# Graph attention on one core: the second layer's transposes, projection and sums in another order and in other PSUM banks

## Chip, cores and metric

The kernel runs on one core of a Trainium2 chip. The metric is the device time of one execution in microseconds (us); the time of a kernel is the median of its runs. The engines are TensorE (PE, with its weight loads shown as PEld), VectorE (DVE), ScalarE (ACT), GpSimd (POOL) and SyncE (SP); PE writes its results to PSUM[...].

## What is computed

Two graph attention layers, each with a residual and a layer norm, over 3327 nodes with 1024 features and a sparse symmetric adjacency matrix. The second layer has one head:

```python
    def _L1_gnn_ref(input, adj, W, a1, a2):
        h = input @ W
        f1 = h @ a1
        f2 = h @ a2
        e = jax.nn.leaky_relu(f1 + f2.T, negative_slope=ALPHA)
        scores = jnp.where(adj > 0, e, neg)
        attention = jax.nn.softmax(scores, axis=1)
        h_prime = attention @ h
        return jax.nn.relu(h_prime)
    ...
    x = _layernorm(x + _L0_gnn_ref(x, adj, L0_gnn_W, L0_gnn_a_src, L0_gnn_a_dst), axis=-1)
    x = _layernorm(x + _L1_gnn_ref(x, adj, L1_gnn_W, L1_gnn_a1, L1_gnn_a2), axis=-1)
```

The first layer (`_L0_gnn_ref`) is the same with eight heads of 128 features, without the relu.

## The kernel before, in words

The nodes are padded to 26 tiles of 128. The kernel has three stages. The first (0 to about 450 us) projects x with W of layer 0 and finds the edges of each node as lists of indices. The second is layer 0, the third layer 1; both are run by the function `pipeline`, over 26 tiles of target nodes. Everything stands in the order in which the program issues it (`manual_schedule`): no scheduler reorders it. Each engine runs its own instructions in that order, and the waits between engines come from what each instruction reads and writes. A PSUM tile is followed as a whole in these waits: L981 on DVE waits for L951 on ACT although the two touch different slices of `way`.

For each tile the edges come in five steps, b = 0 to 4. Steps 0 to 3 hold four groups of 128 edges each, every group for 32 targets; step 4 (`end`) holds one group of 128 edges for all 128 targets. One step of layer 1's class `Target` consists of:

- `fetch` (L803 in `gather`): indirect DMAs, issued by POOL, that gather the source nodes' rows of `y_d` into one of five buffers `src` (or two buffers `end`), four per step and one for the end. The next tile's step b is fetched just after this tile's sums of step b.
- `weights` (L981, L982, L984, DVE): the edges' attention weights, computed in the PSUM tile `way`, result in `es`. They are computed one step ahead of the sums.
- `sums` (L993, PE): `es` times the gathered rows, accumulated in three PSUM tiles `acc` (the columns are cut in three, taken in the order 2, 0, 1). The profile counts a float32 matmul twice: 24 per step, 6 for the end.

Once in a tile, in step 2, `prepare` makes the next tile's row R: PE transposes the nodes' scores (L949), ACT takes the exponential into a slice of `way` (L951), DVE marks the targets (L819, L823) and SP loads the tile's own rows `y` (L956). At the start of the next tile `close` (L1001 to L1010) divides the sums by the row sums and gives `z`.

What remains of a tile, `finish`, is a generator and is run in pieces between the sums of the next tile: four transposes of `z` and ACT's copy into `xT` (L176 and L179 in `transposed`) as the first piece, the other four as the second, and then per half of the output columns the eight products with W in four pieces (L1025; two products, in the profile's count four, per piece), followed by L1028 on DVE, which takes the relu and adds the residual. The layer norm of the output is a second generator, `settle` (L192 to L199, with a square root on ACT for which ACT loads another table, and the store L1036), and runs in the queue `ahead`.

`pipeline(kind, late, behind, get)` says how many pieces run where: `behind[b]` pieces after the sums of step b, and `late` pieces after `close`, just ahead of the sums of step 0. A tile has 10 pieces. So that the first tile's pieces fall in the same places as the others', a dummy of `range(1)` stands ahead of it in the queue.

PSUM's eight banks are given out by tag in `Phase`: A (5) for the sums of both layers, S (1) for layer 0's row sums `den` and for the projection's result `mm`, T (1) for all transposes, E (1) for `way`. `way` has 512 columns: two slices of 128 for R of this and the next tile, a third for the weights, and a fourth that layer 1 doesn't use.

Of the kernel before, what the change touches and what calls it, by code (L numbers as in the profile page):

```python
# [19 lines left out]
P = 128  # L20
# [6 lines left out]
def kernel(  # L27
# [49 lines left out]
    CUTS = (0, 342, 684, D + 1)  # L77
# [79 lines left out]
    class Phase:  # L157
# [7 lines left out]
        def bank(self, tag, shape, name, dt=F32):  # L165
            return self.psum.tile(shape, dt, tag=tag, name=name, bufs=self.banks[tag])
# [286 lines left out]
    with ExitStack() as own, tc.manual_schedule():  # L453
        ph = Phase(own, "proj", {"A": 2, "S": 1, "T": 2})
        pool, bank = ph.pool, ph.bank
# [205 lines left out]
        for t in range(3, NT):  # L661
# [3 lines left out]
            if t == 12:  # L665
                n, own = NT - 1, pool.tile([P, NT], I32, bufs=1, name="own")
# [27 lines left out]
        tr = bank("T", [1, P], "trc")  # L694
# [46 lines left out]


    def sparse(own):
        ph = Phase(own, "sparse", {"A": 5, "S": 1, "T": 1, "E": 1})
        pool, bank, sbuf = ph.pool, ph.bank, ph.sbuf
        NS = 5
        srcs = [pool.tile([P, NG, HG], F32, bufs=1, name=f"src{n}") for n in range(NS)]
# [8 lines left out]
        way = bank("E", [P, HALF], "way")  # L756
# [30 lines left out]
        def run(work, steps=1):  # L787

            while work and steps:
                try:  # L790
                    next(work[0])
                    steps -= 1
                except StopIteration:
                    work.popleft()
# [19 lines left out]
        def marks(t):  # L814

            m = NB - 1
            oh = sbuf("oh", [P, m * GT + P], 2)
            parts = oh[:, : m * GT].rearrange("p (b t) -> p b t", t=GT), oh[:, m * GT :]
            nc.vector.tensor_tensor(  # L819
                parts[0], io_t[:, :GT].unsqueeze(1).to_broadcast([P, m, GT]),  # L820
                tgt[:, t, :m].unsqueeze(2).to_broadcast([P, m, GT]), OP.is_equal,
            )
            nc.vector.tensor_scalar(parts[1], io_t, tgt[:, t, m:], None, op0=OP.is_equal)  # L823
            return parts

        class Layer0:
# [5 lines left out]
            def prepare(self):  # L832
                self.re = listed.pop(self.t)
                self.oh, self.oh2 = marks(self.t)
                self.y = ys[self.t % 3]
                load_rows(self.y[:, :D], x, self.t)
                self.h = sbuf("own", [P, HW0], 2)
                nc.sync.dma_start(self.h, h0_d[self.t * P : (self.t + 1) * P, :])
# [13 lines left out]
            def begin(self):  # L852
                self.acc = [bank("A", [P, 4, DH], "acc") for _ in range(2)]
# [86 lines left out]
        class Target:  # L940
# [4 lines left out]

            def prepare(self):
                t = self.t
                tr = bank("T", [P, P], "tr")
                nc.tensor.transpose(tr, r1.s[:, t, :].to_broadcast([P, P]), ident)  # L949
                self.r = way[:, (t % 2) * P : (t % 2 + 1) * P].rearrange("p (g t) -> p g t", g=NG)  # L950
                nc.scalar.activation(  # L951
                    self.r.rearrange("p g t -> p (g t)"), tr, AF.Exp, scale=1 - SLOPE
                )
                self.oh, self.oh2 = marks(t)
                self.res = ys[t % 3]
                nc.sync.dma_start(self.res, y_d[t * P : (t + 1) * P, :])  # L956
# [12 lines left out]
                self.src[b] = gather(y_d, HW, self.t, b)  # L969

            def begin(self):
                self.acc = [bank("A", [P, CUTS[1]], "acc1") for _ in range(3)]

            def weights(self, b):
                s = self.src[b]
# [62 lines left out]
        def pipeline(kind, late, behind, get):  # L1038

            tiles = [kind(t) for t in range(NT)]
            work = deque()
            get(0)
            tiles[0].prepare()
            for b in range(EB + 1):
                tiles[0].fetch(b)
            tiles[0].weights(0)
            for t, tg in enumerate(tiles):  # L1050
                tg.begin()
                for b in range(EB + 1):
                    if b == 0 and t:
                        tiles[t - 1].close()
                        run(work, late)
                    if b == 0 and t + 1 < NT:
                        get(t + 1)
                    if b == 2 and t + 1 < NT:
                        tiles[t + 1].prepare()
                    if b == 0:  # L1060
                        tg.own()
                    if b < EB:
                        tg.weights(b + 1)
                    elif t + 1 < NT:
                        tiles[t + 1].weights(0)
                    tg.sums(b)
                    if t + 1 < NT:
                        tiles[t + 1].fetch(b)
                    run(work, behind[b])
                    if t or b:  # L1070
                        run(ahead)
                if t == 0 and late:
                    work.append(iter(range(1)))
                work.append(tg.finish())
            tiles[-1].close()
            run(work, late)
            run(ahead, -1)
            run(work, -1)
            run(ahead, -1)

        with tc.manual_schedule():
            pipeline(Layer0, 0, (1, 1, 1, 1, 1), get_edges)
            pipeline(Target, 1, (2, 2, 2, 2, 1), lambda t: None)


    def by_pairs(own):
# [119 lines left out]
    with arm.Else():  # L1206
        with ExitStack() as own:
            sparse(own)
# [23 lines left out]
```

## Time and profile before

| | us |
|---|---|
| median of 3 runs (lowest to highest) | 1957.28 (1956.42 to 1968.05) |
| the profiled execution | 1903.19 |
| its span, first to last instruction | 1901.5 |
| PE busy | 1518.5 (80%) |
| DVE busy | 1146.6 (60%) |
| POOL busy | 1030.2 (54%) |
| ACT busy | 546.6 (29%) |
| L1025, layer 1's projection on PE | 383.3 |
| L993, layer 1's sums on PE | 206.2 |
| L803, gathers of y_d on POOL | 415.7 |

The profile is one execution on the chip. The span is what its records cover, and the execution's own time lies 1.7 us above it; the median of the runs lies 54.1 us above that. A row of the timeline gives start, duration, engine, line, operation, written and read tiles, and in brackets how long the engine stood idle ahead of it and which instruction's end released it. The chain of waits follows the work that ended last back from the end: each piece is either an instruction or what it waited for. Counts in a row are those of the hardware's instructions.

### The profile page before, as it was taken

What the parts mean: (1) busy time and instruction counts of PE and PEld (TensorE: products, weight loads), DVE (VectorE), ACT (ScalarE), POOL (GpSimd) and SP (SyncE); (2) the same over time, 40 slices, a digit from 0 to 9 for tenths busy, and PEclk for the clock granted to TensorE, in tenths of its full rate; (3) what the DMA queues carried; (4) which work ended last, traced back from release to release, by engine and by line L of the source; (5) the groups of instructions that cost most, each with busy time, mean ns of one, the idle gap of its engine ahead of it and who ended that gap; (6) DMA issues with size and microseconds to landing.
All of it is one profiled execution on the core that took longest, in us unless ns stands there. A gap on an engine that the chain in (4) does not pass through costs nothing.

```text
span 1901.5 us, 38079 instructions
## 1 busy us (share of the span) xinstructions
PE 1518.5 (80%) x14663; PEld 902.4 (47%) x14663; DVE 1146.6 (60%) x3058; ACT 546.6 (29%) x1422; POOL 1030.2 (54%) x1391
## 2 busy tenths in 40 slices
PE   8799999999266555656556565399999999999997
PEld 5465556666255554545545454144444444444443
DVE  6699999986386665666666666244444444444442
ACT  5544455542022222222222222012222212222220
POOL 4322222220576666676676764677766667666650
PEclk9899999999678777787788877699999999999999
DMA  7656455411899999999999997899999999999980
GB/s 184 101 133 131 100 99 99 88 62 39 325 373 404 396 392 394 366 405 392 386 392 389 394 376 273 332 398 410 400 372 382 380 378 369 359 371 373 366 326 33
DMA packets 171068, 567.76 MB, mean 299 GB/s; under 512 B 27690, under 2 KB 34346, under 8 KB 170878
## 3 DMA queue, kind: packets, MB, share of 16 engines
q0 software_dynamic: 131056, 455.68, 67.6%
q1 hardware_dynamic: 39822, 109.56, 15.4%
q8 instruction: 118, 1.93, 0.4%
q14 instruction: 72, 0.59, 0.1%
HBM read 578.85 MB, written 42.97 MB: 327 GB/s over the span
## 4 chain that ended last, share of the span: by engine, by line
PE 52%; DMA 24%; DVE 12%; ACT 6%; issue 4%; POOL 2%; SPq 0%; DVEq 0%; ACTq 0%; POOLq 0%
DMA src<-h_d,idx 20%; PE mm L1025 20%; PE acc L993 12%; PE mm L479 12%; DVE e L870 3%; PE acc L898 3%; ACT junk L311 3%; PE tr L176 2%; POOL src L803 2%; DMA src<-y_d,idx 2%; DVE pr L931 1%; PE acc L882 1%; DMA wt<-in_L_gnn_W_dram 1%; ACT xT L179 1%; PE xp L411 1%
## 5 line engine op out<-in xcount | busy, mean ns | idle before, releaser
L803 POOL DMA_INDIRECT src<-h_d,idx x416 | 441.1, 1060 | 209.1 <-PE acc L898 58.0
L803 POOL DMA_INDIRECT src<-y_d,idx x416 | 415.7, 999 | 221.6 <-PE acc L993 96.3
L898 PE MATMUL acc<-src,e 128*32 128x128 f32 x6656 | 278.5, 337 | 253.6 <-DVE e L870 253.5
L479 PE MATMUL mm<-wt,xT 128*128 128x347 f32 (+1 forms) x1248 | 402.3, 469 | 3.3 <-DMA wt<-in_L_gnn_W_dram 2.9
L1025 PE MATMUL mm<-wt,xT 128*128 128x512 f32 x832 | 383.3, 604 | 0.8 <-DVE o L1028 0.8
L898 PEld LDWEIGHTS acc<-src,e 128*32 128x32 f32 x6656 | 234.8, 137 | 311.3 <-DVE e L870 284.3
L479 PEld LDWEIGHTS mm<-wt,xT 128*128 128x128 f32 x1248 | 228.3, 192 | 106.0 <-issue 4.2
L1025 PEld LDWEIGHTS mm<-wt,xT 128*128 128x128 f32 x832 | 152.2, 190 | 199.5 <-issue 179.1
L993 PE MATMUL acc<-src,es 128*32 128x342 f32 (+1 forms) x2496 | 206.2, 464 | 33.8 <-DVE es L984 31.0
L870 DVE TENSOR_TENSOR e<-oh,way 128x1024 f32<-128x1024 f32 x130 | 158.7, 1221 | 63.2 <-ACT w L868 62.8
L993 PEld LDWEIGHTS acc<-src,es 128*32 128x32 f32 x2496 | 71.6, 111 | 158.6 <-issue 112.9
L868 ACT ACTIVATE w<-way 128x32 f32<-128x32 f32 (+1 forms) x130 | 24.6, 189 | 407.7 <-DVE way L866 395.6
L1028 DVE SCALAR_TENSOR_TENSOR o<-mm,y 128x512 f32<-128x512 f32 x52 | 35.9, 691 | 166.2 <-PE mm L1025 166.2
L1007 ACT ACTIVATE z<-y,ri 128x342 f32<-128x342 f32 (+1 forms) x78 | 39.5, 570 | 313.9 <-DVE ri L1003 313.9
L865 DVE TENSOR_TENSOR way<-src,re 128x32 f32<-128x32 f32 x104 | 20.8, 200 | 175.1 <-DMA src<-h_d,idx 157.6
L179 ACT ACTIVATE xT<-tr 128x512 f32<-128x512 f32 x104 | 59.4, 596 | 151.0 <-PE tr L176 150.9
L981 DVE TENSOR_TENSOR way<-way,src 128x128 f32<-128x128 f32 x104 | 31.1, 299 | 90.0 <-ACT way L951 44.2
L850 ACT ACTIVATE own<-own,es 128x128 f32<-128x128 f32 x208 | 63.6, 388 | 57.4 <-DVE es L847 57.4
L311 ACT ACTIVATE junk<-ad 128x3328 uint8<-128x3328 uint8 x26 | 78.4, 3014 | 2.5 <-POOL ad L308 2.5
L882 PE MATMUL acc<-end,e 128*128 128x128 f32 x416 | 67.7, 328 | 13.3 <-DVE e L870 13.3
L296 POOL CAST mvs<-r 128x8 bf16<-128x8 f32 x26 | 6.0, 232 | 122.8 <-ACT r L295 122.8
L335 POOL TENSOR_TENSOR place_of<-cnt 128x1 f32<-128x1 f32 x26 | 4.9, 190 | 121.0 <-ACT cnt L328 101.5
(188 smaller groups left out, 1959.7 us busy)
## 6 DMA issues: line engine op xcount, KB each, us to landing
h_d<-ht SPq DMA_DIRECT2D x26, 520.0 KB
own<-h_d SPq DMA_DIRECT2D x26, 520.0 KB
y_d<-y SPq DMA_DIRECT2D x26, 514.0 KB
y<-y_d SPq DMA_DIRECT2D x26, 514.0 KB
x<-in_x_dram SPq DMA_DIRECT2D x25, 512.0 KB
y<-in_x_dram SPq DMA_DIRECT2D x25, 512.0 KB
out_dram<-o SPq DMA_DIRECT2D x25, 512.0 KB
ad<-in_adj_dram POOLq DMA_DIRECT2D x25, 415.9 KB
```

The source lines that it names most:

```text
L176: nc.tensor.transpose(tr[:, k, :], src[:, (4 * g + k) * P : (4 * g + k + 1) * P], ident)
L179: nc.scalar.activation(part, tr, AF.Copy)
L311: nc.scalar.activation(junk, ad, AF.Copy, accum_out=self.deg)
L479: nc.tensor.matmul(acc, xT[t][:, k, :], wt[:, k, CUTS0[c] : CUTS0[c + 1]], start=k == 0, stop=k == KT - 1)
L803: nc.gpsimd.indirect_dma_start(out=s[:, g, :w], out_offset=None, in_=table[:, :], in_offset=bass.IndirectOffsetOnAxis(ap=idx[:, t, b * NG ...
L850: nc.scalar.activation(hn, hn, AF.Copy, scale=es[:, n : n + 1])
L870: nc.vector.tensor_tensor(e, oh.unsqueeze(2).to_broadcast([P, ng, H, wide]), wp.unsqueeze(3).to_broadcast([P, ng, H, wide]), OP.mult,)
L882: nc.tensor.matmul(self.acc[h // 4][:, h % 4, :], e[:, 0, h, :], rowsof[:, 0, h, :], start=False, stop=h % 4 == 3,)
L898: nc.tensor.matmul(self.acc[h // 4][g * GT : (g + 1) * GT, h % 4, :], e[:, g, h, :], rowsof[:, g, h, :], start=first and h % 4 == 0, stop= ...
L993: nc.tensor.matmul(self.acc[c][to, :m], es[:, g, :], s[:, g, CUTS[c] : CUTS[c + 1]], start=b == 0, stop=b == EB,)
L1007: nc.scalar.activation(z[:, cut], self.res[:, cut], AF.Copy, scale=ri[:, 1:2])
L1025: nc.tensor.matmul(acc, xT[:, k, :], wt1[:, k, half], start=k == 0, stop=k == KT - 1)
```

## The change

It has five edits, in layer 1 but for the banks, which both layers share. The bank counts become 4 for A and 2 for S. R's transpose writes the unused fourth slice of `way` in place of a bank T tile. The three `acc` tiles are taken in the order in which the sums use them. The pieces are spread as `late` 2 and `behind` (1, 1, 2, 2, 2) in place of 1 and (2, 2, 2, 2, 1): the two halves of the transposes now fall behind the sums of steps 0 and 1, the first half of the projection behind those of steps 2 and 3, the second behind the end and ahead of the next tile's sums. The dummy is as long as `late`.

```diff
     def sparse(own):
-        ph = Phase(own, "sparse", {"A": 5, "S": 1, "T": 1, "E": 1})
+        ph = Phase(own, "sparse", {"A": 4, "S": 2, "T": 1, "E": 1})
...
             def prepare(self):
                 t = self.t
-                tr = bank("T", [P, P], "tr")
+                tr = way[:, 3 * P :]
                 nc.tensor.transpose(tr, r1.s[:, t, :].to_broadcast([P, P]), ident)
...
             def begin(self):
-                self.acc = [bank("A", [P, CUTS[1]], "acc1") for _ in range(3)]
+                self.acc = {c: bank("A", [P, CUTS[1]], "acc1") for c in (2, 0, 1)}
...
                 if t == 0 and late:
-                    work.append(iter(range(1)))
+                    work.append(iter(range(late)))
                 work.append(tg.finish())
...
             pipeline(Layer0, 0, (1, 1, 1, 1, 1), get_edges)
-            pipeline(Target, 1, (2, 2, 2, 2, 1), lambda t: None)
+            pipeline(Target, 2, (1, 1, 2, 2, 2), lambda t: None)
```

## The prediction, on record before the changed kernel ran

> **What bounds the kernel now.** I began with the busy time by window, to see which stage the edited lines lie in (columns: window, length, busy time and count of PE, PE weight loads, DVE, ACT, POOL, then granted clock, DMA share, GB/s):
>
> ```profile
> 450.00:1198.00 748.00, 444.23 (x8282) 364.49 (x8280) 467.28 (x1135) 176.90 (x525) 469.00 (x449) 0.79 0.94 362
> 1198.00:1260.00 62.00, 40.16 (x250) 15.54 (x251) 16.48 (x54) 4.95 (x12) 47.12 (x48) 0.81 1.01 396
> 1260.00:1847.50 587.50, 571.67 (x3294) 245.37 (x3295) 261.88 (x759) 134.27 (x230) 394.31 (x395) 1.00 0.99 378
> 1847.50:1901.50 54.00, 41.57 (x183) 17.89 (x182) 16.71 (x43) 5.69 (x11) 0.00 (x0) 0.94 0.08 30
> ```
>
> Layer 1 is the last three rows. From 1260 to 1847.5 PE is busy for 571.67 of 587.50 us; before that, for some two tiles, it is not. Next the chain of work that ended last, for tile 2 of layer 1; its period is the same in every later tile (start us, us, what):
>
> ```profile
> 1260.04 1.86 PE acc L993 x24
> 1261.90 0.60 PE tr L176 x4
> 1262.50 0.02 issue
> 1262.53 0.61 ACT xT L179
> 1263.13 0.04 issue
> 1263.18 0.66 PE tr L176 x4
> 1263.83 1.86 PE acc L993 x24
> 1265.69 3.63 PE mm L1025 x8
> 1269.33 0.11 PE tr L949
> 1269.44 1.86 PE acc L993 x24
> 1271.30 3.63 PE mm L1025 x8
> 1274.93 1.86 PE acc L993 x24
> 1276.79 3.63 PE mm L1025 x8
> 1280.42 1.73 PE acc L993 x6
> 1282.15 3.43 PE mm L1025 x8
> 1285.58 1.86 PE acc L993 x24
> ```
>
> The period is 1285.58 - 1260.04 = 25.54 us. All of it is PE except 0.02 + 0.61 + 0.04 = 0.67: the second half's transposes wait until ACT has emptied the one T bank. Also, eight projection matmuls cost 3.63 after a block of sums with 32-column weights, but 3.43 after the end block. The waits of PE in that window are one row, so nothing else is to be had there:
>
> ```profile
> PE tr L176 <- ACT xT L179: 15.8, 23, 0.7
> ```
>
> Last, the timeline around the start of layer 1 and in the tail (start, duration, [idle before, releaser]):
>
> ```profile
> 1242.37 0.30 DVE L981 TENSOR_TENSOR way<-way,src 128x128 f32<-128x128 f32 x1 [4.20 <-DMA src<-y_d,idx]
> 1876.65 8.73 PE L1025 MATMUL mm<-wt,xT 128*128 128x512 f32 x16
> 1886.16 7.13 PE L1025 MATMUL mm<-wt,xT 128*128 128x512 f32 x16 [0.79 <-DVE o L1028]
> ```
>
> In tile 1 the weights still wait for gathers (4.20); in the tail the second half's matmuls wait 0.79 for the only S bank.
>
> [...] DVE L981 waits 44.2 us in 23 times for ACT L951, although the two use different slices of way. So the moved R transpose must wait for DVE's last use of way. [...] clock records of 3.41 us at 0.5, one of them right after an idle of 2.75 in the tail. [...] The trace has the 1.28 us, and the next ACTIVATE 0.01 us after it; I use 1.28.
>
> **The change, part by part.** T is the start of a tile's first sums.
>
> *Order on PE.* The built order of the changed kernel gives, per tile: sums0, 4 transposes, sums1, 4 transposes, R, sums2, mm8, sums3, mm8, end, mm16 (in the profile's count). With the rows above: 1.86 + 0.60 + 1.86 + 0.60 + 0.11 + 1.86 + 3.63 + 1.86 + 3.63 + 1.73 + 3.43 + 3.42 = 24.59 us. (The final eight follow their like: 8 x 0.427 = 3.42.) Saved: 25.54 - 24.59 = 0.95, say 0.94: 0.67 of ACT wait, 0.06 of the transposes after it, 0.21 because one changeover less has the 0.2.
>
> *Is the wait really covered?* The first half's transposes end at T + 2.46, ACT takes 0.61: free at 3.1. The second half's start at 4.32, behind sums1 (1.86). Cover to spare 1.2. Should it go, 0.67 comes back.
>
> *ACT.* Its order becomes xT half, sqrt table load, sqrt, xT half, exp table load, L951. Second xT half at 4.96 to 5.56, the exp load (which in the built program now waits for the R transpose) 5.56 to 6.84, L951 to 7.1. The second half is needed at the second mm8, T + 12.4: free of charge. DVE's weights for step 3, which wait for L951, run 7.15 to 8.1 (three of 0.3 us); sums3 wants them at 10.5. Before, they ran from T + 9.8.
>
> *R's transpose in way's bank.* New wait: L949 behind DVE's weights for step 2. Queued behind it on PE is sums2, which needs the same weights, so only their lateness counts. The timeline of one tile of before (T = 1515.47, less 0.07 for what the chain calls start) has:
>
> ```profile
> 1519.81 0.29 DVE L984 TENSOR_TENSOR es<-way,oh 128x128 f32<-128x128 f32 x1
> ```
>
> That ends at T + 4.63; DVE's order up to there does not change, and it starts from the last L1028, which still runs at T. PE wants it at T + 4.92: margin 0.29, less some 0.05 of semaphore. Cost 0; if 0.3 us were missing, 7 us in all. Sums1 needs its weights at 2.46, they end at 2.02.
>
> *Two S banks.* In steady state one bank was never waited for (0.8 us, once, in the tail). In the new order only the 1.73 of the end block lies between the halves, L1028 takes 0.69: no wait either way. In the tail the 0.79 goes.
>
> *Four A banks.* A tile takes three, so the next tile's second and third bank are those of which close reads the first and second. Close ends about 4.5 us after the end block starts; the 16 matmuls behind it last until 8.6. Cost 0 (before, too, one bank was shared). Layer 0 takes two per tile: four suffice. Its den rows show no PE wait that a second S bank could remove: 0.
>
> *L1028 of the first half* moves ahead of the next tile's first weights on DVE, which are wanted 7 us later: 0.
>
> *POOL and SP* keep their order. A gather waits for the sums five slots earlier; those now end 0, 1.4, 4.4, 4.4 us earlier in the tile, while src1 is wanted at the same T + 1.1, src2 at T + 3.7, src3 2.5 us earlier. From the landings of each gather in the trace, the slack to its weights is 7.5 to 13 us from tile 9 on; in tile 3 it is 3.8, 1.3 and 2.2 for src1 to src3. One tile takes 17 issues of 1.30 = 22.1 us of POOL, and in bytes about 378 GB/s x 25.5 us = 9.6 MB, which at the 410 seen in early tiles is 23.5 us (estimate). Both are under 24.59. The y load moves with prepare, 2.5 us earlier in the tile; SP has room.
>
> *The start.* Tile 1 is paced by landings: src2 lands at 1242.2, its weights end at 1243.3. Before, PE filled 1240.15 to 1243.78 with mm8. Now it has only four transposes (to 1240.8) and idles 2.6 us; the mm8 comes after the end block. So: sums2 1243.5, mm8, sums3 1249.0, mm8, end 1254.5, mm16 from 1256.2, tile 2 at 1263.1 instead of 1260.04: 3.1 us lost. By the grid of the clock records the window 1239.2 to 1242.6 would be 45% busy. One at 39% was followed by half clock, one at 57% not, so half clock for 3.4 us is open: 0 to 1.7 us more. I take 0.85. Slack after that: tile 3's src3 lands at 1293.1 and is wanted at 1287.7 + 7.3 = 1295.0; later tiles have more.
>
> *Sum.* 24 periods (tiles 2 to 25) x 0.94 = 22.6; start -3.1 and -0.85; tail +0.8. Net 19.4: span 1901.5 to 1882.1, profiled execution 1903.19 to 1883.8. The runs' median lies 54.1 us above that execution, and nothing in the profile shows where; I carry the difference over unscaled: 1957.28 - 19.4 = 1937.9, which is 0.99% less. One per cent, 19.6 us, is about what a measurement of this kernel can tell from no change, so the forecast sits on that line.
>
> **The rivals.**
> *Transfers take over.* DMA share is 0.99 and the runs are slower than the profile. For it: 23.5 us against 24.59 is 4% of room; if the missing 54 us are slow transfers in layer 0's 748 us (7%), a tile costs 25.1 in transfers and gains 0.4, while the start's loss drowns in the wait for them: 24 x 0.4 + 0.8 = 10.4 us, 1947. Against it: in the profile slack grows from tile to tile.
> *The clean sum without the clock loss, or with a longer one:* 1937.0 or 1938.7; part of the forecast.
> *A thin margin fails.* R's wait or sums1's weights lie 0.1 to 0.5 us late, as any delay on DVE passes the 0.24 left: 2 to 12 us given back, 1940 to 1950.
> *Slower.* The same place, further out: if PE's wait for way also covered weights or table loads behind step 2 (L951's exp load, 1.28, or weights 3), each R would hold PE by over a microsecond. It decides from 0.94 + 0.24 = 1.2 us late; at 2.2 us, 24 us lost, 1981. Against it: the built order has only DVE's count on L949, and what stands behind it there doesn't come before.
> *The change does nothing:* PE's order does change, and no other engine has the 0.67 waiting; I give it nothing apart from these.
>
> **How the numbers follow.** Forecast 0.70 (1935 to 1942 with the scatter of the runs), transfers 0.12, thin margin 0.12, slower 0.06. The forecast is over 1% faster about two times in three given that scatter and the unknown clock: 0.47, and with a little of the rest 0.48. Slower 0.06, the remaining 0.46 within. Range 1927 to 1950: it leaves out the slower case and the ends of the others; below, as much as the scatter and a few tenths per changeover (0.2 x 24 = 5 us) could give.
>
> **What would show it.** PE's row "tr L176 <- ACT xT L179" gone but in the tail; a period of 24.6 in the chain; ACT L951 at T + 7; tile 2 starting at about 1263 to 1265; the 0.79 before the last 16 matmuls gone. Wrong if L949 or sums1 shows a DVE wait in each tile, if DVE L981 waits for gathers after tile 5, or if the period stays above 25.

## The result and the profile after

| | before | changed |
|---|---|---|
| median of 6 runs each, first comparison | 1960.4 us | 1991.67 us |
| ratio (95% interval) | | 1.0172 (1.0147 to 1.0198) |
| profiled execution | 1903.19 us | 1988.58 us |
| its span | 1901.5 us | 1986.5 us |

The changed kernel was 1.7% slower in the first comparison; forecast was 1% faster. The table holds a clue to the cause: for the changed kernel the profiled execution agrees with the runs, for the kernel before it lies 57 us under them. The two profiles may therefore not show the same conditions, and cannot simply be subtracted.

The busy time by window of the changed kernel (columns as before):

```profile
450.00:1198.00 748.00, 562.65 (x7948) 384.83 (x7946) 442.91 (x1088) 170.70 (x515) 465.50 (x452) 0.82 0.96 357
1260.00:1847.50 587.50, 552.08 (x3034) 234.26 (x3034) 237.80 (x699) 120.70 (x210) 367.29 (x369) 0.98 0.94 351
```

The first row is layer 0, where the order of the instructions is the same as before: PE is nonetheless busy for 562.65 us instead of 444.23 with fewer matmuls done (7948 against 8282), and layer 1's first gather is issued at 1231.2 us instead of 1198.6. In layer 1, the chain of waits shows a tile's time:

```profile
1500.20 1.86 PE acc L993 x24
1502.06 0.59 PE tr L176 x4
1502.65 1.86 PE acc L993 x24
1504.51 0.59 PE tr L176 x4
1505.10 0.11 PE way L949
...
1517.92 6.87 PE mm L1025 x16
1524.79 1.29 PE acc L993 x16
```

From 1500.20 to 1524.79 the tile runs as forecast, in 24.59 us: the wait for ACT between the transposes is gone and nothing waits for R. But of the 23 tiles from tile 2 to tile 24 it is the only one that does; their mean period is 27.2 us. The loss of the others lies, with few exceptions, in one place: the sums of step 3, the fourth block of sums, and the end of the products just ahead of it. In the tile that begins at 1364.29 that block reads:

```profile
1374.86 0.77 PE acc L993 x7
1375.69 0.45 PE acc L993
1376.13 0.28 issue
1376.41 0.75 PE acc L993 x2
1377.16 0.65 issue
1377.81 1.40 PE acc L993 x14
```

Here matmuls stand apart within a block, with "issue" between them: the engine waits for nothing that the profile shows. Such pauses are called stalls below. In layer 0, where no line of the change stands, the chain of the changed kernel has them too:

```profile
1196.06 0.27 PE acc L898
1196.33 0.46 issue
1196.79 0.28 PE acc L898
```

Between two successive matmuls of L898 more than 0.25 us pass 389 times in the trace of the changed kernel, start to start, and never in the profile of before.

### The profile page after: what moved, and what is told of

Same layout as the page of the kernel before. It is cut to its first block, busy times and chain, and to the rows that moved or that the text cites. A ratio compares the mean times of both kernels' runs of the same rounds, so it can differ in the third digit from the quotient of the medians.

```text
span 1986.5 us, 38080 instructions
## 1 busy us (share of the span) xinstructions
PE 1686.6 (85%) x14663; PEld 950.4 (48%) x14663; DVE 1140.5 (57%) x3058; ACT 545.9 (27%) x1422; POOL 1025.5 (52%) x1391
## 4 chain that ended last, share of the span: by engine, by line
PE 73%; issue 11%; DVE 6%; ACT 5%; DMA 4%; POOL 1%; another core or an unknown queue 0%; DVEq 0%; SPq 0%; POOLq 0%; ACTq 0%
PE mm L1025 17%; PE acc L898 17%; PE acc L993 13%; PE mm L479 12%; PE acc L882 5%; PE acc L890 3%; ACT junk L311 3%; PE tr L176 2%; DMA src<-h_d,idx 2%; DMA wt<-in_L_gnn_W_dram 1%; PE den L907 1%; PE xp L411 1%; DMA src<-y_d,idx 1%; DVE st L192 1%; ACT away L384 0%
## 5 line engine op out<-in xcount | busy, mean ns | idle before, releaser
L803 POOL DMA_INDIRECT src<-h_d,idx x416 | 436.4, 1049 | 241.1 <-PE acc L898 105.1
L898 PE MATMUL acc<-src,e 128*32 128x128 f32 x6656 | 377.8, 306 | 165.8 <-issue 154.4
L898 PEld LDWEIGHTS acc<-src,e 128*32 128x32 f32 x6656 | 238.0, 122 | 321.0 <-issue 280.1
L1025 PE MATMUL mm<-wt,xT 128*128 128x512 f32 x832 | 375.6, 600 | 0.0
L993 PE MATMUL acc<-src,es 128*32 128x342 f32 (+1 forms) x2496 | 242.9, 469 | 70.0 <-issue 37.0
L993 PEld LDWEIGHTS acc<-src,es 128*32 128x32 f32 x2496 | 80.7, 111 | 213.5 <-issue 179.0
L882 PE MATMUL acc<-end,e 128*128 128x128 f32 x416 | 94.3, 418 | 1.6 <-DVE e L870 1.6
L882 PEld LDWEIGHTS acc<-end,e 128*128 128x128 f32 x416 | 87.5, 320 | 2.3 <-DVE e L870 1.7
L890 PE MATMUL acc<-own,ident 128*128 128x512 f32 x104 | 69.7, 757 | 0.0
```

What stands on the lines that cost most here:

```text
L803: nc.gpsimd.indirect_dma_start(out=s[:, g, :w], out_offset=None, in_=table[:, :], in_offset=bass.IndirectOffsetOnAxis(ap=idx[:, t, b * NG ...
L882: nc.tensor.matmul(self.acc[h // 4][:, h % 4, :], e[:, 0, h, :], rowsof[:, 0, h, :], start=False, stop=h % 4 == 3,)
L890: nc.tensor.matmul(self.acc[b - 1].rearrange("p h d -> p (h d)"), ident, self.h[:, (b - 1) * HALF : b * HALF], start=False, stop=False,)
L898: nc.tensor.matmul(self.acc[h // 4][g * GT : (g + 1) * GT, h % 4, :], e[:, g, h, :], rowsof[:, g, h, :], start=first and h % 4 == 0, stop= ...
L993: nc.tensor.matmul(self.acc[c][to, :m], es[:, g, :], s[:, g, CUTS[c] : CUTS[c + 1]], start=b == 0, stop=b == EB,)
L1025: nc.tensor.matmul(acc, xT[:, k, :], wt1[:, k, half], start=k == 0, stop=k == KT - 1)
```

## The experiments

Three theories stood at the start. **A:** the new order of the pieces stalls PE. **B:** the banks, or R in way's bank, do it. **C** (D in later texts): the stalls belong to the chip that a run came to, and the profile of before was of another one. The runs came to several chips, and the kernel before, which ran beside each, took a median of 1898 to 1905 us on three of them (called the first kind below: chips 0, 4, 6) and of 1959 to 1984 on three others (the second kind: chips 7, 8, 10); the first comparison, at 1960, looks like the second. Chip 4 came up twice, half an hour apart, and was of the first kind both times; each other chip came up once, so whether the kind belongs to the chip or to its state at that time is not shown. A period is the mean of the 23 from tile 2 to tile 25. Two further theories on the stalls came later: **T**, they hang on the gathers, and **N**, on the density of short PE instructions.

**Before again, and the change in parts (chip 4).** `e0_before` is the kernel before.

> The kernel before, unchanged, for a profile beside those of the changed kernels. Theory C (the profile of before that the prediction rested on is quicker than that kernel's usual runs, and the stalls of PE without a releaser are in it too): a profiled execution near 1955 us, not 1903, with the additional 50 us in PE rows that name no releaser, in layer 0 or 1. Theories A and B (the stalls come with the change): near 1903 in the profile, tile period 25.5 us in layer 1, no such stalls. Ratio 1.00 within half a per cent in either.

Measured: 1897.34 us, 0.9995 (0.9985 to 1.0005), profiled 1897.84; period 25.5 us, no stalls. The profile of before was no lucky execution: it shows what the kernel does on a chip of this kind. The numbers are those expected of A and B, but the kernel's other runs on this chip took 1898 us too, where the first comparison had 1960: before itself differs between chips by 60 us, which no branch had foreseen.

`e1_banks`, on the changed kernel:

```diff
-            pipeline(Target, 2, (1, 1, 2, 2, 2), lambda t: None)
+            pipeline(Target, 1, (2, 2, 2, 2, 1), lambda t: None)
```

> The changed kernel with the pieces placed as before (late 1, behind 2,2,2,2,1): only the banks, R in way's bank and the order of acc are changed. Theory A (the order of the pieces makes the loss): ratio 1.00 to before, within 0.5%. Theory B (the banks make it: the second S bank or the four A banks delay layer 0, or R in way's bank delays layer 1): 1.010 to 1.017, with layer 0 ending up to 30 us later than in before's run of this job.

Measured: 0.9995 (0.9986 to 1.0004), period 25.5. Banks and R's place alone cost and give nothing on this chip.

`e2_pieces`, on the kernel before:

```diff
-                    work.append(iter(range(1)))
+                    work.append(iter(range(late)))
...
-            pipeline(Target, 1, (2, 2, 2, 2, 1), lambda t: None)
+            pipeline(Target, 2, (1, 1, 2, 2, 2), lambda t: None)
```

> The kernel before with the changed kernel's places of the pieces (late 2, behind 1,1,2,2,2) and a dummy as long as late, but with five A banks, one S bank, R in the T bank. R then waits for ACT's second copy, about 0.7 us per tile, 17 us in all. Theory A: as slow as the changed kernel or slower, ratio 1.015 to 1.025, layer 0 as in before. Theory B: 1.00, that is the 0.7 per tile regained in R and nothing lost.

Measured: 1.0009 (1.0000 to 1.0018). The period stays 25.5: PE's only wait row in layer 1 is now that of R for ACT's second copy,

```profile
PE tr L949 <- ACT xT L179: 15.8, 23, 0.7
```

with the same 15.8 us as the one it replaces. The parts work only together: the split frees PE of the wait, and with R's place in way's bank it does not come back at L949 (in `h_after`, below, PE has no wait row between 1260 and 1835 us). Theory A's loss of 1.5 to 2.5% did not come; but as no kernel stalls on this chip, these runs do not yet decide between A and B.

`e3_even`, on the changed kernel:

```diff
-            pipeline(Target, 2, (1, 1, 2, 2, 2), lambda t: None)
+            pipeline(Target, 2, (1, 3, 2, 2, 0), lambda t: None)
```

> The changed kernel with pieces at late 2, behind 1,3,2,2,0: halves of the transposes still in different steps, but eight projection products after each of the steps 1, 2, 3 and the end, as before, in place of sixteen in one stretch. Theory A (sums and gathers crowd in the first part of a tile and the stretch of sixteen leaves the buffers unemptied): the period is 24.8 us, ratio 0.99. Theory B: as the changed kernel, 1.01 to 1.02. Theory C: the same stalls as in before, ratio 0.99 to 1.00.

Measured: 1871.71 us against 1898.18, 0.9852 (0.9833 to 0.9870), period 24.59: the fastest of the complete kernels on this chip.

**The changed kernel on both kinds of chip.** `g_after` (the changed kernel), `g_even` (as e3_even) and `g_before` (before) came to chip 7.

> The changed kernel again, unchanged. Theory D (a state of the chip or of the program's place in memory, in which PE is without instructions for a while: it was there in the first comparison, where the kernel before too ran at 1957 us against 1898 in the last job): where the kernel before runs at about 1900, the changed kernel has a period of 24.6 us in layer 1, no stalls without a releaser, and a ratio of 0.986 to 0.990. Theory A (the stretch of sixteen, or the crowding of sums, stalls PE by itself): a period near 27.1 and a ratio of 1.01 to 1.02 on this chip as well.

> The same as e3_even, for a comparison on the same chip as g_after. Theory D: 0.985 where before runs at 1900, within 0.3% of the changed kernel; if the chip is one where before runs at 1957, a smaller gain or a loss, like the changed kernel's. Theory A: 0.985, and clearly below the changed kernel.

> The kernel before, for a profile from the same chip as the other two. Theory D: at 1900 us no stalls of PE without a releaser in layer 1; at 1957 us such stalls in its profile too, of some 2 us per tile or in layer 0. Theory A: none, on either chip.

Measured: before 1959.14; changed 1992.84, 1.0163 (1.0134 to 1.0191), period 27.3; g_even 1959.53, 1.0006 (0.9989 to 1.0023), period 26.0; g_before 1.0003 (0.9989 to 1.0017), its period 25.76. All three reach layer 1's first gather at 1231.0 to 1233.1, against 1191.1 to 1195.5 for the four kernels on chip 4: some 37 us of the 60 by which this chip is slower are lost ahead of layer 1, and not through the change. In the 23 periods g_before loses 5.0 us against e0_before, nearly all in three tiles; g_even loses 32.4 against e3_even, g_after 61.1 against the same kernel on chip 4 (`h_after`, next). PE's waits in g_before between 1290 and 1840 us seem to hold, beside the known one, one that names nothing:

```profile
PE tr L176 <- issue: 9.6, 14, 0.7
PE tr L176 <- ACT xT L179: 6.3, 7, 1.4
```

The two rows are most likely one wait: together 21 times, once a tile, with mostly the same 0.7 us. On a chip of this kind part of the records that name a releaser is missing (in the trace of the first comparison 822 of ACT's 1128 counts are there, in the profile of before 1115), so a wait that names nothing is not yet a stall. Pauses within a block of matmuls, as above, have no such wait ahead of them.

`h_after`, the changed kernel on chip 4, and `i_after` on chip 0, with `i_pieces` (as e2_pieces):

> The changed kernel once more. On a chip on which the kernel before takes about 1898, theory D (the loss belongs to chips on which PE also stalls in layer 0) gives a period of 24.6 us and a ratio of 0.986 to 0.990; theory A (the order stalls PE on any chip) 1.01 to 1.02. On a chip on which before takes 1957 both give 1.015 again.

> The changed kernel, as the measure for the other three on the same chip: 1.016 and a period of 27.2 where before takes 1957, 0.989 and 24.6 where it takes 1900.

> As e2_pieces (the changed kernel's places of the pieces, the banks of before, R in the T bank). On a chip where before takes 1957: if the order alone brings the stalls, a period of 27 to 28 and a ratio of 1.016 to 1.025; if they come with R in way's bank, 25.5 to 26 and 1.00. Where before takes 1900: 1.001 again.

Measured: h_after 1883.40 against 1903.98, 0.9889 (0.9870 to 0.9908), period 24.64, no stalls; i_after 0.9922 (0.9905 to 0.9940), 24.62; i_pieces 1.0037 (1.0025 to 1.0050), 25.49. Theory D's branch held, though i_after and i_pieces came out 0.3% higher than expected: the same program is 0.8 to 1.1% faster on one kind of chip and 1.6% slower on the other. A as stated, a loss on any chip, has fallen; so has B. But on a chip of the second kind neither e1_banks nor e2_pieces ever ran. That the order plays a part there follows from g_even and g_after, which have the same banks; whether the banks or R's place add to it is not known.

**What the stalls hang on.** In `few`, layer 1's sums become one matmul per cut (the rest of the line as before):

```diff
-                    for g in range(NG if b < EB else 1):
-                        to = slice(g * GT, (g + 1) * GT) if b < EB else slice(0, P)
                         nc.tensor.matmul(
-                            self.acc[c][to, :m], es[:, g, :], s[:, g, CUTS[c] : CUTS[c + 1]],
+                            self.acc[c][:, :m], es.rearrange("p g t -> p (g t)"), s[:, 0, CUTS[c] : CUTS[c + 1]],
```

In `quarter`, layer 1 gathers one group per step:

```diff
-            for g in range(NG if b < EB else 1):
+            for g in range((NG if w == HW0 else 1) if b < EB else 1):
                 nc.gpsimd.indirect_dma_start(
```

> The changed kernel, but layer 1's sums use the first of the four gathered groups alone, as one matmul with 128 columns of weights in place of four with 32: the sums of the other three groups are left out. PE's time for a step stays (1.73 us against 1.86), its instructions for it fall from 24 weight loads and 24 matmuls to 6 and 6; all gathers are still made. On a chip with stalls, theory N ([...] three steps of sums follow one another with only transposes between) expects the stalls gone and a period of 24.0 to 24.3 us. Theory T (the transfers of the gathers hold PE up) expects the period to stay at 27. On a chip without stalls, 24.0 to 24.3 in both.

> The changed kernel with only one of the four groups of each step gathered in layer 1: three quarters of the rows are left out, and what an earlier gather left in the buffers is used in their place. On a chip with stalls, theory T expects them gone, a period of 24.6 us. Theory N expects them to stay, a period of 27. On a chip without stalls, 24.6 in both, and tile 1 without its wait for gathers.

> As h_few (layer 1's sums of three of the four groups left out, one matmul with 128 columns of weights in place of four with 32; all gathers made). On a chip where before takes 1957: theory N (too many short instructions in a burst) a period of 24 us in layer 1; theory T (the transfers) a period of 26.5 to 27. On a chip where before takes 1900: 23.9 again, which tells nothing.

> As h_quarter (three of the four groups of each step are not gathered in layer 1; older rows are used). On a chip where before takes 1957: theory T a period of 24.6 us; theory N 27. On a chip where before takes 1900: 24.6 again.

> As h_few (layer 1's sums of three of the four groups left out; a quarter of PE's short instructions, all gathers made). On a chip where before takes 1957: theory N (dense short PE instructions) a period near 24 us and the stalls gone in layer 1; theory T (the gathers, their transfers or the records of their landings) 26.5 to 27. On a chip where before takes 1900: 23.9.

> As h_quarter (three of four groups not gathered in layer 1, older rows used; all PE instructions). On a chip where before takes 1957: theory T 24.6 us per tile and all records of landings there in layer 1; theory N 27. On a chip where before takes 1900: 24.6.

These six came to chips 4, 0 and 6, of the first kind, and so settled nothing about the stalls. `few`: 0.9813 (0.9791 to 0.9836), 0.9812 (0.9793 to 0.9832), 0.9806 (0.9730 to 0.9882), period 23.97. `quarter`: 0.9766 (0.9746 to 0.9786), 0.9775 (0.9755 to 0.9795), 0.9781 (0.9714 to 0.9848), period 24.59, tile 1 without its wait. That `quarter` has the changed kernel's period (24.59 against 24.64 and 24.62) with a DMA share of 0.39 instead of 0.98 (h_quarter and h_after, 1260 to 1847.5) says that on these chips transfers don't set it.

`k_quarter`, the same as h_quarter, came to chip 8, of the second kind:

> As h_quarter (three of four groups not gathered in layer 1, older rows used; all PE instructions). On a chip where before takes 1957: theory T (gathers, their transfers or the records of their landings) a period of 24.6 us; theory N (dense short PE instructions) 27. On a chip where before takes 1900: 24.6.

Measured: 1907.67 against 1983.71, 0.9599 (0.9503 to 0.9695), period 24.59 in every tile, no stall in layer 1, while layer 0, untouched, has them as on chip 7 (PE busy for 544.37 us from 450 to 1198; g_after 557.41, h_after 444.02). T's branch held, and N falls as it was stated: all short instructions of the sums were there, and without the gathers they bring no stall. That their density plays no part is not shown: `few` never came to a chip of the second kind, and there g_before, g_even and g_after, with the same gathers and the same instructions, lose 5.0, 32.4 and 61.1 us; they differ in their order and, the first from the other two, in the banks.

`l_narrow` keeps all gathers and cuts their bytes to a quarter:

```diff
+            if w == HW:
+                w, table = HW // 4, table[:, :].rearrange("n (a w) -> (n a) w", a=4)
+            else:
+                table = table[:, :]
...
-                    out=s[:, g, :w], out_offset=None, in_=table[:, :],
+                    out=s[:, g, :w], out_offset=None, in_=table,
```

> The changed kernel with all of layer 1's gathers, each moving 257 instead of 1028 elements per row (rows cut to a quarter and taken from other places; the rest of the buffer is older data). On a chip where before takes 1957 or more: if the stalls hang on the bytes moved, a period of 24.6 us without stalls; if they hang on the number of gathers and landings, 26.5 to 27. On a chip where before takes 1900: 24.6, and tile 1 less late than with full rows[...].

It came to chip 10, of the second kind: 2012.78 against 1983.31, 1.0166 (1.0089 to 1.0244), period 27.4, about as with full rows (27.3). The windows of layer 1 (the 550 us from 1290 on) side by side, h_after, g_after, k_quarter and l_narrow in this order, one row from each trace:

```profile
1290.00:1840.00 550.00, 549.73 (x3231) 239.99 (x3230) 255.31 (x747) 131.15 (x224) 372.62 (x373) 1.00 0.99 385
```

```profile
1290.00:1840.00 550.00, 521.18 (x2868) 222.83 (x2866) 226.81 (x663) 117.38 (x202) 342.12 (x344) 1.00 0.94 347
```

```profile
1290.00:1840.00 550.00, 550.00 (x3210) 239.65 (x3211) 247.70 (x737) 130.85 (x225) 116.53 (x113) 1.00 0.44 138
```

```profile
1290.00:1840.00 550.00, 508.98 (x2847) 222.62 (x2847) 219.71 (x650) 113.88 (x197) 343.07 (x343) 0.99 0.40 115
```

The last two move nearly the same bytes (138 and 115 GB/s) and have the DMA engines busy to the same extent (0.44 and 0.40). The one with 113 gathers does 3210 matmuls in the window, the one with 343 does 2847. (In g_after and l_narrow the window still holds part of the start, so the periods, 24.59 and 27.4, are the better measure.) So on such a chip the stalls follow the number of gathers, or what goes with it (POOL's issues and the records of their landings), not their bytes. Two runs and one trace of each, on two chips, carry this.

## Why the prediction was wrong

**The step that failed** is the sum's last: "The runs' median lies 54.1 us above that execution, and nothing in the profile shows where; I carry the difference over unscaled". It takes for granted that what the profile shows, and so the saving of 0.94 us in each period, holds in the runs too. But the profile has the marks of a chip of the first kind (a period of 25.54, no pauses in L898), and the runs those of the second (before at 1960). There the 54 us are no constant around the profiled work: between e0_before on chip 4 and g_before on chip 7 the same program loses 38.6 us ahead of layer 1's first gather, 18.0 from there to tile 2, 5.0 in the 23 periods and 1.7 after them. And there the change costs time: its 23 periods take 627.8 us instead of 592.4, so 35.4 are lost where 23 x 0.94 = 21.6 were to be saved (start and tail give 1.7 back, net 33.7).

**What gives way on such a chip** is a margin of the part on ACT. The prediction has ACT's second copy start at T + 4.96 and DVE's weights for step 3 end at T + 8.1, over 2 us before PE wants them at 10.5. On chip 4 this is so: T + 5.0 and 8.2. In the trace of the first comparison, in a tile that begins at 1418.55 and whose second four transposes end at T + 5,

```profile
1426.47 0.60 ACT L179 ACTIVATE xT<-tr 128x512 f32<-128x512 f32 x1 [3.25 <-PE acc L993]
1428.38 0.26 ACT L951 ACTIVATE way<-way 128x128 f32<-128x128 f32 x1
1429.41 0.29 DVE L984 TENSOR_TENSOR es<-way,oh 128x128 f32<-128x128 f32 x1
1429.76 0.77 PE L993 MATMUL acc<-src,es 128*32 128x341 f32 x7 [0.63 <-DVE way L982]
```

the copy starts at T + 7.9 and the weights end at T + 11.1, too late for PE. In 22 of the 23 tiles of g_after the copy starts 2.2 to 3.8 us after its transposes, in h_after and k_quarter always 0.04; the tile in which it comes on time is the one without a loss. This points to a late signal rather than a late ACT: in the records of the semaphore that PE counts up, a count stands 0.02 us ahead of the copy (median), as in h_after. In g_before L951, which waits for PE's L949, is as late (T + 12.2 instead of 9.5, medians), but the weights behind it end at 13.5 and PE wants them at 14.9: the old order hides what the new one does not. This accounts for a part of the loss: in g_after the sums of step 3 start 0.6 us later on average (T + 11.2, in h_after 10.5), and then last 2.0 us longer through the pauses within them.

**"Transfers take over"** took the runs' distance from the profile seriously, but it named bytes (its 25.1 us a tile would have been a gain), and l_narrow shows that a quarter of the bytes changes nothing. **"Slower"** alone had the direction, and named instructions that do come late, L951 and the weights of step 3; but it had them hold R, and on chip 7 none of PE's waits between 1290 and 1840 us is at L949.

**On a chip of the kind that the profile shows the sum held.** From the first gather of layer 1 to the end, e0_before takes 700.7 us and h_after 682.6: 18.1 saved, 19.4 forecast. By term:

- *The period:* 23 tiles took 587.4 and take 566.6, so 20.8 saved where 23 x 0.94 = 21.6 were forecast; 24.64 us each against the 24.59 of the sum.
- *The start:* tile 2 begins 65.6 us after the first gather, before 60.9: 4.7 lost, forecast 3.1 and 0 to 1.7 for the clock. Both came: the timeline of h_after in tile 1 has the idle of 2.7 and the step of sums at half speed, 3.57 us where the next steps take 1.93:

```profile
1244.10 0.32 PE L949 MATMUL way<-ident,sd 128*128 128x128 f32 x1 [2.67 <-DVE es L984]
1244.35 3.57 PE L993 MATMUL acc<-src,es 128*32 128x341 f32 x24
```

- *Last tile and tail:* 50.3 instead of 52.3, 2.0 saved, forecast 1.7. The tail's projection is one piece with no wait for an S bank:

```profile
1860.60 13.75 PE mm L1025 x32
```

- *The margins:* in a tile of h_after that begins at 1512.25,

```profile
1516.59 0.29 DVE L984 TENSOR_TENSOR es<-way,oh 128x128 f32<-128x128 f32 x1
...
1516.99 0.27 PE L949 MATMUL way<-ident,sd 128*128 128x128 f32 x1
...
1519.10 0.26 ACT L951 ACTIVATE way<-way 128x128 f32<-128x128 f32 x1
```

the weights end at T + 4.63, L949 follows at 4.7 to 4.9 and L951, behind ACT's table load of 1.28 us (1517.81 to 1519.09), ends at 7.1, all as worked out; the margin of 0.29 was enough.

**What e3_even does better** is the start: its tile 2 begins 61.4 us after the first gather instead of 65.6, since eight projection matmuls stand again where tile 1 waits for its gathers, and its period is the same 24.59. On chip 7 it stalls too (26.0), less than the changed kernel (27.3), and only equals the kernel before.

**What stays open.** Why what waits for PE starts late on these chips, and whether that or something behind both makes PE pause within a block, was not settled. A count of the trace's records gives a hint. In the profile of before 345 of 371 landings from 1300 us on left 16 records each, and none left more; at 16 each, 442 gathers leave 7072 in each layer. On chip 4 the trace of the changed kernel holds 7041 in layer 1 and 6972 in layer 0, on chip 7 only 2726 and 3337. In k_quarter, whose layer 1 doesn't stall, 1825 of 2080 are there in layer 1, and 3357 in layer 0. But g_before has lost as many in layer 1 (2688 are left) and hardly stalls in its periods (5.0 us lost in 23): on such chips records are missing where all gathers run, whether or not PE loses time. What makes the records go missing, and whether it has to do with PE's pauses, was not shown: every run was recorded, and missing records, late signals and pauses may come about separately. A lack of fetched instructions is unlikely: in g_after the 26 packets of the larger instruction queue (q8, 118 packets in the profile of before against 72 of q14; taken as PE's, which that page does not show) that land in these 23 tiles do so anywhere from T + 0.5 to T + 28, while the loss stays in the sums of step 3 and just ahead of them in nearly every tile.

## What to carry to other kernels

Before a profile's durations are used to forecast a ratio of runs, compare its execution with the runs: a gap of 3% which no row shows is a part of the program that is unknown, not an offset, and nothing says how a change acts on it. When work moves closer to what it feeds, note how much margin the old order left there: before could take L951 2.7 us late at no cost, the changed kernel could not. When a wait on PE is removed by spreading work, place the freed work where the engine would otherwise wait for data at the start: on a chip without stalls e3_even and the changed kernel have periods of 24.59 and 24.64 us, and differ by the start (tile 2 at 61.4 and 65.6 us after the first gather). A split of a double step pays only if what stands behind it leaves that buffer too: either half of this change alone gave nothing on a chip without stalls (0.9995 and 1.0009).

## What was not expected of the hardware

The same program ran 3 to 4% apart on two kinds of chip (1898 to 1905 and 1959 to 1984 us for the kernel before). On the second kind, ACT's second copy, which waits for PE, started 2.2 to 3.8 us after the transposes that it needs in 22 of 23 tiles of the changed kernel (g_after), and PE paused within blocks of matmuls; both were gone in layer 1 with a quarter of the gathers (k_quarter), and a quarter of the bytes did not help (l_narrow). In h_after, half speed followed a PE idle of 2.67 us in tile 1 (3.57 us instead of 1.93 for the next step of sums), while an idle of 3.2 us in the tail (1856.8 to 1860.0) was followed by full speed (32 matmuls in 13.75 us). The clock records of this run stand on a grid of 3.41 us: the first idle leaves one window of the grid 22% busy, the second is split over two, which are 55% and 64% busy.
